# A PSUM column for an exclusive-or on VectorE, and ScalarE's one-hots in the plain parts of a graph layer

## The chip, the core and the metric

The kernel runs on one core of a Trainium2 chip. A core has five engines with queues of their own: TensorE (PE; its weight loads are listed as PEld), VectorE (DVE), ScalarE (ACT), GpSimd (POOL) and SyncE (SP, which issues most DMAs). Each works through its own instructions in order; semaphores tie them together. SBUF is the large on-chip memory of 128 partitions, PSUM the smaller one into which TensorE writes. The metric is the device time of one execution in microseconds.

## What is computed

A graph of 12500 nodes with 128 features each and 412500 directed edges, sorted by target node `dst` (200000 random pairs in both directions, and a loop at each node). For each edge the difference of its two nodes' rows is taken, a small network makes a gate of it, and gated differences are summed at the target:

```python
theta = x[dst] - x[src]
w = sigmoid(relu(theta @ W1 + b1) @ W2 + b2)
agg = segment_sum(w * theta, dst)
indeg = segment_sum(ones, dst)
y = agg + indeg * (x @ W4 + b4)
out = layernorm(x + y)
```

Since `theta @ W1` is `x[dst] @ W1 - x[src] @ W1`, a table of both products and rows can be made once, and an edge then needs one row of it, fetched by `src`.

## The kernel before

**Table.** The first stage (`chunk`, `table_chunk`) multiplies all rows by W1 and writes a table `z` to DRAM, a row being `x @ W1` and `x` side by side (1 KB).

**Sets.** Edges are worked in sets, one to a *part* of the program. Sets 0 to 17 are the *plain* sets of 1024 consecutive edges (`PLAIN = 18`, `K = 8` groups of 128 edges on the partitions); sets 0 to 3 (`NH = 4`) run on rows of `x` while the table is still being made. Sets 18 to 275 hold 1532 edges each; of those, up to 512 go by way of *hot* regions, and 1024 slots by gathers. For each set GpSimd issues eight gathers (`gather`, an indirect DMA of 128 rows, L401) into one of five buffers `zbuf`, four parts ahead in the plain parts and three in the later ones.

**A part.** VectorE takes the difference of the gathered half and the target's half (L948 in plain parts, L951 in later ones), clamps and multiplies by W2 (L956) and sums to logits `lg` (L962). ScalarE takes the sigmoid (L975) and weighs the rows (`weigh`, L986; `weigh_rest`, L993), which also frees the gather buffer. TensorE sums the weighed rows into windows of 104 target nodes (`add_up`, L1158), multiplying by one-hot matrices `ow` of the target's place in its window. `one_hot_w` (L926) makes these on VectorE, as `iota == rel`, two tiles of 4 x 104 columns for a plain set and one for a later set; four tiles `ow` exist. `iota` was copied to the PSUM tile `fix` at the start, as was W2 for L956. The places `rel` of the plain sets lie in the tile `rel0`, of BF16.

**Placement.** Which edges of a later set go to which hot region or gather slot is found on the chip by `place(i, ...)`, once for each of five groups of up to 64 sets (the last has two sets), with one list to a partition and 767 edges to a list. It goes through 32 regions (`HR`). For each it changes the bits of its keys by an exclusive-or with a constant (L583, 128x767, 31 times per group), takes the eight largest (`max`, L586), and marks them taken (L589). Further steps compact the lists (L640 to L682) and end in the indices `src_i` (L713, ScalarE), on which the gathers of these sets depend. `place` is a generator. `spend` and `advance` run some of its steps in each part, against a credit by part and a table of costs by kind of step, `"x": 0.5` for the exclusive-or. Group 0 (sets 18 to 81) is placed during the table stage and the plain parts and must be done before part 14 (`assert steps[0] is None`); groups 1 to 4 are placed one after the other in parts of the set group before.

**Hot tables.** In parts 4 to 9 `table_terms` (L1087, L1096) splits rows of `x` into three BF16 terms: once in parts 4 to 7, twice in parts 8 and 9. It goes through the PSUM banks `px` and `pd`. `place` uses the two `px` banks as scratch too (`where[0] = wide`), and both take them in turn. In later parts `hot_tiles` (L1039, VectorE) makes one-hots for the hot regions.

**Order.** From part 0 on, all of PE, DVE and ACT stand in the order in which `early_part` (plain parts) and `part` (later parts) write them. In `early_part` ScalarE gets, in this order: the copies of hot products (L1069), in odd parts the totals of a block (L1213, L820, L1232, L1234), whatever `logits` issues, the sigmoid, the weighting, in even parts the next block's plain one-hots (`plain_one_hots`, L860, L861), and the table terms.

Of the kernel before, what the change touches and what calls it, by code (L numbers as in the profile page):

```python
# [9 lines left out]
F32 = mybir.dt.float32  # L10
BF16 = mybir.dt.bfloat16
F16 = mybir.dt.float16
I32 = mybir.dt.int32
U16 = mybir.dt.uint16
AF = mybir.ActivationFunctionType
OP = mybir.AluOpType
# [4 lines left out]
P = 128  # L21
D = 128
K = 8
J = K // 2
BE = K * P
SUB = 2
WB = 104
# [12 lines left out]
NH = 4  # L40
# [3 lines left out]
PLAIN = FIRST + MORE  # L44
HS = 16
HR = 32
# [19 lines left out]
WL = HL + 1  # L66
# [7 lines left out]
FIELD = 19  # L74
# [10 lines left out]
def gnn_resnorm(  # L85
# [37 lines left out]
    nc = tc.nc  # L123
# [16 lines left out]
    while n0 < N:  # L140
# [5 lines left out]
    const = ctx.enter_context(tc.tile_pool(name="const", bufs=1))  # L146
# [8 lines left out]


    placed = {0: (const.tile([P, K, PLAIN], I32, name="src0"),
                  const.tile([P, K, PLAIN], BF16, name="rel0"), None)}

    def set_of(s):  # L160

        s0 = 0 if s < PLAIN else PLAIN + (s - PLAIN) // S2 * S2
        return placed[s0], s - s0
# [106 lines left out]
    iota_row = const.tile([P, P], F32, name="iota_row")  # L270
# [28 lines left out]
    fix = cps.tile([P, 512], F32, name="fix")  # L299
    iota_f = fix[:, :WB].rearrange("p (o m) -> p o m", o=1)  # L300
    w2_b = fix[:, WB:WB + D]
    w2_f = w2_r.rearrange("p (o m) -> p o m", o=1)

    oh_all = const.tile([P, NO * RW], F32, name="oh")
# [18 lines left out]
    def constants():  # L323

        nc.vector.tensor_copy(ident_b, ident)
        nc.vector.tensor_scalar_mul(nident_b, ident, -1.0)
        nc.vector.tensor_scalar_mul(wneg, wts[:, 0, :], -1.0)
        nc.scalar.activation(fix[:, :WB], iota_row[:, :WB], AF.Copy)

        nc.scalar.activation(w2_b, w2_r, AF.Copy)  # L330
        half = const.tile([P, 1], F32, name="half")
        nc.vector.tensor_scalar(half, iota_p, float(HALF), -float(HALF), op0=OP.is_ge, op1=OP.mult)
        nc.vector.tensor_add(half, half, iota_p)
        nc.vector.tensor_scalar(mine, half, float(SW), None, op0=OP.is_lt)
        nc.vector.tensor_scalar(away, half, float(SW), -2.0, op0=OP.is_gt, op1=OP.mult)
        nc.vector.tensor_mul(half, half, mine)
        nc.vector.tensor_sub(away, away, half)
        nc.vector.tensor_scalar_mul(less, mine, -1.0)

        nodes = const.tile([P, HT], F32, name="nodes")  # L340
        node_c = const.tile([P, 1], F32, name="node_c")
        nc.vector.tensor_scalar(node_c, iota_p, float(HT), None, op0=OP.mult)
        nc.vector.tensor_scalar(nodes, iota_row[:, :HT], node_c, None, op0=OP.add)

        most = const.tile([P, 1], F32, name="most")
        nc.vector.memset(most, float(SW + HKL))
        apart = const.tile([P, PM], F32, name="apart")
        nc.vector.tensor_scalar(apart, iota_row[:, :PM], float(HOT), None, op0=OP.mult)
        return nodes, (apart, most)
# [18 lines left out]
    def pairs(s):  # L368
        return J if s < NF else JT
# [130 lines left out]
    def place(i, scratch, es, ed, bb, dp):  # L500
# [4 lines left out]
        s0, n, full = sets[i]  # L505
# [3 lines left out]
        v = nc.vector  # L509
# [17 lines left out]
        for r in rows:  # L527
            v.scalar_tensor_tensor(b[r, 3:4], c[r, 2:3], float(NOT - WB + 1), c[r, 18:19],
                                   op0=OP.add, op1=OP.add)
# [39 lines left out]
        bits = left.bitcast(I32)  # L569
# [10 lines left out]
        tops = ep.tile([P, WL], F32, name="ed")[:, :HKL].rearrange("p (r e) -> p r e", e=HE)  # L580
        for r in range(HR):
            if r:
                v.tensor_scalar(bits, bits, ((r - 1) ^ r) << FIELD, None, op0=OP.bitwise_xor)  # L583
                yield "x"
            eight = tops[:, r, :]
            v.max(eight, left)  # L586
            v.tensor_scalar(eight, eight, FLOOR, None, op0=OP.max)
            yield "k"
            v.match_replace(left, eight, left, TAKEN)  # L589
            yield "k"  # L590
# [5 lines left out]
                        op0=OP.bitwise_xor, op1=OP.bitwise_and)  # L596
# [38 lines left out]
        for j in range(NC):  # L635
# [10 lines left out]
            else:  # L646
                v.memset(odd[:, :1], 0.0)
            v.tensor_tensor_scan(odd[:, 1:], mark, keep, c[:, 5:6] if j else 0.0,
                                 op0=OP.mult, op1=OP.add)
# [5 lines left out]
                                   op0=OP.min, op1=OP.mult)  # L655
# [18 lines left out]
        for r, m in enumerate([1 << r for r in range(MOVES)]):  # L674
            u = ep.tile([P, WL], I32, name="ew" if r % 2 else "et")
            for a in range(0, WL, P * G):
# [10 lines left out]
                        op0=OP.logical_shift_right, op1=OP.bitwise_and)  # L687
# [10 lines left out]
        rel = pp.tile([P, K, S2], BF16, name="rel")  # L698
# [20 lines left out]
    with tc.manual_schedule(engines={SP}), tc.tile_pool(name="work", bufs=2) as wp, tc.tile_pool(  # L719
        name="ps_y", bufs=2, space=bass.MemoryType.PSUM  # L720
    ) as ps_y, tc.tile_pool(
        name="ps_l", bufs=1, space=bass.MemoryType.PSUM
# [196 lines left out]
        def one_hot_w(s):  # L919

            (_, rel, _), i = set_of(s)
            n = pairs(s)
            parts[s]["ow"] = []
            for k0 in range(0, K if s < PLAIN else J, J):
                ow = wp.tile([P, J, WB], F32, name="ow", bufs=4)
                nc.vector.tensor_tensor(  # L926
                    ow[:, :n], iota_f.to_broadcast([P, n, WB]),
                    rel[:, k0:k0 + n, i:i + 1].to_broadcast([P, n, WB]), op=OP.is_equal)
                parts[s]["ow"].append(ow)

        def logits(s):
# [4 lines left out]
            if s < NH:  # L936
                one_hot_w(s)
                for i, h in enumerate(y):
                    w2 = w2_r.rearrange("p (o d) -> p o d", o=1).to_broadcast([P, J, D])
                    nc.vector.scalar_tensor_tensor(h, h, 0.0, w2, op0=OP.max, op1=OP.mult)  # L940
                    nc.vector.tensor_reduce(lg[:, i * J:(i + 1) * J, 0], h, AX.X, OP.add)
                return
# [16 lines left out]
            if s % SUB == 0:  # L959
                one_hot_w(s)  # L960
            for at in tiles:
                nc.vector.tensor_reduce(lg[:, at, 0], h[:, at, :], AX.X, OP.add)  # L962
            if s % SUB:
                one_hot_w(s)
# [343 lines left out]
        with after(done[1]):  # L1308
            place_first_dst(0, FIRST, ps_l, dst_f)
            nodes, hot_c = constants()  # L1310
            start_of(0, FIRST)

        where = [lambda: ps_l.tile([P, P * G], F32, name="pa")]
        steps = [place(0, lambda: where[0](), *loaded), "k"]

        def advance(kinds, n=1):
# [130 lines left out]
        groups, firsts, i = [], {}, 0  # L1447
# [47 lines left out]
        def part(s):  # L1495
# [6 lines left out]
            if s in edges:  # L1502
                i, loaded = edges.pop(s)
                assert steps[0] is None
                steps[:] = place(i, lambda: where[0](), *loaded), "k"
# [253 lines left out]
```

## Time and profile before

| | |
|---|---|
| Median of 3 runs (lowest to highest) | 2941.33 us (2940.52 to 2944.18) |
| Profiled execution | 2943.8 us |
| Its span, first to last instruction | 2942.0 us |
| VectorE busy | 2380.3 us (81%) |
| ScalarE busy | 2123.8 us (72%) |
| GpSimd busy | 2164.5 us (74%) |
| TensorE busy | 2548.2 us (87%) |
| First gather by placed indices | at 269.25 us |
| End of the last gather | 2915.45 us |

How to read the rows: a group's row has line, engine, operation, output<-inputs by tile names, shapes, `x` its count, then busy us, mean ns of one, and the idle time just before with what ended it. A row of the timeline has start, duration, engine, line, operation, and in brackets the idle time before it and its releaser. A row of waits has who waited for whom, total us, times, and the longest. A row of stretches has its length, then the busy time and count of PE, PEld, DVE, ACT and POOL, the granted TensorE clock, the DMA share and GB/s. A row of one line has the least, median and greatest duration in ns. "issue" is time for which the profile shows no releaser. A busy share says nothing on whether the gaps of an engine can be used.

### The profile page before, as it was taken

How to read it: one execution, taken by the hardware profiler on the slowest of the kernel's cores; microseconds unless marked ns; L12 is line 12 of the kernel's file. 1: busy time of each engine (PE TensorE's matmuls, PEld its weight loads, DVE VectorE, ACT ScalarE, POOL GpSimd, SP SyncE). 2: the span in 40 equal slices, each digit the busy share in tenths (PEclk: the TensorE clock that was granted, in tenths of full speed). 3: DMA queues.
4: the chain of work that ended last, by engine and by line, in shares of the span. 5: the costliest groups of instructions: out<-in, count | busy, mean ns of one | idle time of the engine just before them, and what ended most of it. 6: DMA issues, size and time to landing. Idle time of an engine off the chain costs nothing.

```text
span 2942.0 us, 59129 instructions
## 1 busy us (share of the span) xinstructions
PE 2548.2 (87%) x18606; PEld 2012.3 (68%) x18606; DVE 2380.3 (81%) x4436; ACT 2123.8 (72%) x6416; POOL 2164.5 (74%) x2213
## 2 busy tenths in 40 slices
PE   6877899988888998998898888898998888888886
PEld 5656677777676777776776666676776666677764
DVE  7899699888957988888558888888568888888654
ACT  6365778767777777677777777776777777677776
POOL 4566777777777777777777777777777777777774
PEclk8688999989999999999999999999999999999998
DMA  8455555555554555554554545454554555555542
GB/s 285 151 153 123 142 139 138 140 135 137 140 146 134 137 140 140 133 141 135 143 150 133 135 133 141 132 141 134 143 142 128 140 132 141 133 138 141 141 134 77
DMA packets 239329, 413.58 MB, mean 141 GB/s; under 512 B 63423, under 2 KB 147226, under 8 KB 237470
## 3 DMA queue, kind: packets, MB, share of 16 engines
q0 software_dynamic: 105280, 286.93, 35.3%
q1 hardware_dynamic: 131756, 116.40, 15.3%
q10 hardware_dynamic: 1970, 6.40, 0.7%
q8 instruction: 148, 2.42, 0.3%
q14 instruction: 175, 1.43, 0.2%
HBM read 388.57 MB, written 20.94 MB: 139 GB/s over the span
## 4 chain that ended last, share of the span: by engine, by line
PE 38%; ACT 19%; DVE 15%; DMA 11%; issue 7%; POOL 1%; DVEq 0%; SPq 0%; ACTq 0%; POOLq 0%
PE pa L1158 14%; DMA zbuf<-z,src_i 10%; DVE zbuf L951 5%; PE y L893 5%; PE pd L1055 5%; ACT wx L993 5%; PE px L1119 4%; ACT wxh L1131 4%; PE pz L1105 3%; PE pz L1106 3%; PE pz L1122 3%; ACT oh L872 2%; ACT oh L873 2%; ACT xT L1069 1%; ACT a L1213 1%
## 5 line engine op out<-in xcount | busy, mean ns | idle before, releaser
L401 POOL DMA_INDIRECT zbuf<-z,src_i x2060 | 2018.5, 980 | 637.0 <-issue 236.6
L993 ACT ACTIVATE wx<-zbuf,wx 128x128 f32<-128x128 f32 x2060 | 630.2, 388 | 0.0
L1158 PE MATMUL pa<-wx,ow 128*104 128x260 f32 (+1 forms) x2284 | 628.4, 393 | 0.0
L893 PEld LDWEIGHTS y<-y,oh 128*128 128x128 f32 (+1 forms) x2156 | 276.1, 197 | 420.5 <-DVE zbuf L951 378.2
L1055 PEld LDWEIGHTS <-tabs 128*128 128x128 bf16 x6360 | 452.8, 101 | 124.2 <-issue 8.2
L951 DVE TENSOR_TENSOR zbuf<-y,zbuf 128x1024 f32<-128x1024 f32 x258 | 315.1, 1221 | 272.2 <-DMA zbuf<-z,src_i 270.9
L1055 PE MATMUL pd<-of,tabs 128*128 128x128 bf16 (+3 forms) x6360 | 535.2, 223 | 0.0
L1111 ACT ACTIVATE hr<-pz 128x512 f32<-128x512 f32 x258 | 152.9, 593 | 522.9 <-PE pz L1106 522.8
L893 PE MATMUL y<-y,oh 128*128 128x128 f32 (+1 forms) x2156 | 314.7, 291 | 228.7 <-DVE zbuf L951 220.6
L1158 PEld LDWEIGHTS pa<-wx,ow 128*104 128x104 f32 x2284 | 342.8, 179 | 40.6 <-issue 0.4
L962 DVE TENSOR_REDUCE lg<-zbuf 128x8 f32<-128x1024 f32 x273 | 329.8, 1208 | 13.2
L956 DVE SCALAR_TENSOR_TENSOR zbuf<-zbuf,fix 128x1024 f32<-128x1024 f32 x273 | 331.6, 1215 | 9.3
L1158 PE MATMUL pa<-wxh,owh 128*104 128x130 f32 x2064 | 329.0, 296 | 0.0
L1131 ACT ACTIVATE wxh<-pz,wxh 128x128 f32<-128x128 f32 x1032 | 295.2, 369 | 42.1 <-PE pz L1122 35.9
L1105 PE MATMUL pz<-xT,wni 128*128 128x512 f32 x516 | 278.5, 621 | 1.6 <-ACT wxh L1131 1.6
L1158 PEld LDWEIGHTS pa<-wxh,owh 128*104 128x104 f32 x2064 | 274.3, 186 | 0.0
L1119 PEld LDWEIGHTS px<-w_c,hr 128*128 128x128 f32 x2064 | 263.5, 200 | 7.8 <-ACT hr L1111 7.8
L1119 PE MATMUL px<-w_c,hr 128*128 128x1 f32 x2064 | 262.1, 248 | 5.6 <-ACT hr L1111 5.6
L1106 PE MATMUL pz<-oh,y 128*128 128x512 f32 x516 | 264.5, 594 | 0.1
L872 ACT ACTIVATE oh<-to_all,away,mine 128x512 f32<-128x512 bf16 (+1 forms) x257 | 213.6, 831 | 3.1 <-DMA to_all<-off_d 3.1
L1106 PEld LDWEIGHTS pz<-oh,y 128*128 128x128 f32 x516 | 98.2, 191 | 124.3 <-issue 123.4
L1122 PE MATMUL pz<-wni,xT 128*128 128x128 f32 x1032 | 176.3, 297 | 0.0
(304 smaller groups left out, 3595.8 us busy)
## 6 DMA issues: line engine op xcount, KB each, us to landing
to_all<-off_d SPq DMA_DIRECT2D x258, 128.0 KB
zbuf<-z,src_i POOLq DMA_INDIRECT x2060
hot_src<-hot_s SPq DMA_DIRECT2D x228, 128.0 KB
y<-z SPq DMA_DIRECT2D x270, 28.0 KB
xw<-in_x_dram SPq DMA_DIRECT2D x138, 52.0 KB
out_dram<-o SPq DMA_DIRECT2D x138, 52.0 KB
wx<-in_x_dram ACTq DMA_DIRECT2D x12, 512.0 KB
z<-zbuf SPq DMA_DIRECT2D x6, 1024.0 KB
```

What stands on the lines that cost most here:

```text
L401: ins = nc.gpsimd.indirect_dma_start(out=rows_of(s)[:, k, :], out_offset=None, in_=z if s >= NH else x, in_offset=IndirectOffsetOnAxis(ap= ...
L893: nc.tensor.matmul(y[:, j, :], d["oh"][:, (k0 + j) * P:(k0 + j + 1) * P], y_of(s), start=True, stop=True)
L951: nc.vector.tensor_sub(half, yy.to_broadcast([P, 2, n, D]), half)
L956: nc.vector.scalar_tensor_tensor(h[:, at, :], h[:, at, :], 0.0, w2.to_broadcast([P, n, D]), op0=OP.max, op1=OP.mult)
L962: nc.vector.tensor_reduce(lg[:, at, 0], h[:, at, :], AX.X, OP.add)
L993: weighed[0] = nc.scalar.activation(wx[:, k, :D], rows_of(s)[:, k, D:], AF.Copy, scale=wx[:, k, D:D + 1])
L1055: steps_of.append(lambda q=q, i=i, t=t, j=j: nc.tensor.matmul(to[:, q], tabs[:, g, i, q, t, :], of[:, t, q], start=j == 0, stop=j == HT * ...
L1105: nc.tensor.matmul(pz, wneg, xT, start=True, stop=False)
L1106: nc.tensor.matmul(pz, y_of(t), blocks[t // SUB]["oh"][:, BP:], start=False, stop=True)
L1119: nc.tensor.matmul(lgh()[:, t % SUB, q:q + 1], hr[:, at], w2_c, start=True, stop=True)
L1131: nc.scalar.activation(wx[:, q, :D], pz[:, q * P:(q + 1) * P], AF.Copy, scale=wx[:, q, D:D + 1])
L1158: return [lambda i=i, one=one, w=w: nc.tensor.matmul(to if len(w.shape) == 3 else to[:, 0, :], one, w, start=first and i == 0, stop=last a ...
```

## The change

Two things are changed together.

*The exclusive-or.* In groups 1 to 4 of the placement (`if i:`) the instruction with a constant becomes one with two tensor operands, the second being one column of PSUM repeated along the row. Five such columns, with the five constants that occur (1, 3, 7, 15 and 31 shifted left by 19), are set once in the tile `fix`. Group 0 keeps the instruction with a constant. The table of costs is as before.

*One-hots of plain parts.* In sets 4 to 17 ScalarE makes them, as 1 - |rel - iota| clamped at zero: for each of the two tiles four instructions Abs, one to each group of 104 columns (the place `rel` is the bias by partition), and one Relu over the tile in place. `rel0` becomes F32. Sets 0 to 3 and all later sets keep VectorE's comparison.

```diff
     placed = {0: (const.tile([P, K, PLAIN], I32, name="src0"),
-                  const.tile([P, K, PLAIN], BF16, name="rel0"), None)}
+                  const.tile([P, K, PLAIN], F32, name="rel0"), None)}
...
+    steps_c = fix.bitcast(I32)[:, WB + D:WB + D + HR.bit_length() - 1]
...
+        for k in range(HR.bit_length() - 1):
+            nc.vector.memset(steps_c[:, k:k + 1], ((2 << k) - 1) << FIELD)
...
             if r:
-                v.tensor_scalar(bits, bits, ((r - 1) ^ r) << FIELD, None, op0=OP.bitwise_xor)
+                if i:
+                    k = ((r - 1) ^ r).bit_length() - 1
+                    v.tensor_tensor(bits, bits, steps_c[:, k:k + 1].to_broadcast([P, WL]), op=OP.bitwise_xor)
+                else:
+                    v.tensor_scalar(bits, bits, ((r - 1) ^ r) << FIELD, None, op0=OP.bitwise_xor)
                 yield "x"
...
-                nc.vector.tensor_tensor(
-                    ow[:, :n], iota_f.to_broadcast([P, n, WB]),
-                    rel[:, k0:k0 + n, i:i + 1].to_broadcast([P, n, WB]), op=OP.is_equal)
+                if NH <= s < PLAIN:
+                    for k in range(J):
+                        nc.scalar.activation(ow[:, k, :], iota_row[:, :WB], AF.Abs, scale=-1.0,
+                                             bias=rel[:, k0 + k, i:i + 1])
+                    nc.scalar.activation(ow, ow, AF.Relu, scale=-1.0, bias=1.0)
+                else:
+                    nc.vector.tensor_tensor(
+                        ow[:, :n], iota_f.to_broadcast([P, n, WB]),
+                        rel[:, k0:k0 + n, i:i + 1].to_broadcast([P, n, WB]), op=OP.is_equal)
```

## The prediction

> **What bounds the kernel now.** I read the page first (shares and the costliest groups), then GpSimd's own timeline, its waits, the stretches with and without exclusive-ors, and last the plain parts, engine by engine.
>
> ```profile
> span 2942.0 us, 59129 instructions
> PE 2548.2 (87%) x18606; PEld 2012.3 (68%) x18606; DVE 2380.3 (81%) x4436; ACT 2123.8 (72%) x6416; POOL 2164.5 (74%) x2213
> L401 POOL DMA_INDIRECT zbuf<-z,src_i x2060 | 2018.5, 980 | 637.0 <-issue 236.6 <-ACT wx L993 143.3 <-DMA zbuf<-z,src_i 61.3
> ```
>
> By shares TensorE would be the bound and POOL would have a quarter of its time free. The timeline of POOL says otherwise:
>
> ```profile
> 269.25 0.95 POOL L401 DMA_INDIRECT zbuf<-z,src_i  x1 [9.26 <-ACT src_i L713]
> ...
> 979.66 0.94 POOL L401 DMA_INDIRECT zbuf<-z,src_i  x1 [0.30 <-issue]
> ...
> 982.16 0.94 POOL L401 DMA_INDIRECT zbuf<-z,src_i  x1 [0.30 <-ACT hr L1111]
> 983.41 1.55 POOL L401 DMA_INDIRECT zbuf<-z,src_i  x1 [0.30 <-issue]
> ...
> 986.52 1.29 POOL L401 DMA_INDIRECT zbuf<-z,src_i  x1 [0.30 <-ACT sw L1232]
> ...
> 2914.50 0.95 POOL L401 DMA_INDIRECT zbuf<-z,src_i  x1 [0.30 <-issue]
> ```
>
> A gather takes 0.95 us and the next follows after 0.30, whoever is named as releaser. The same 0.30 stands in the waits as the longest wait on the engine that frees gather buffers:
>
> ```profile
> POOL zbuf L401 <- ACT wx L993: 143.3, 470, 0.3
> POOL zbuf L401 <- ACT src_i L713: 9.9, 3, 9.3
> DVE zbuf L951 <- DMA zbuf<-z,src_i: 270.9, 138, 6.5
> ```
>
> So from 269.25 us on POOL never waits for a buffer; VectorE waits for gathers, 138 times. 2060 gathers run from 269.25 to 2915.45 without a break: 2646.2 us, of which 2060 x 1.253 = 2581 is the undisturbed pace and 65 us is gathers that took longer than 0.95. A tail of 26.5 us follows. The time is thus: POOL's start at 269.25, plus 2581, plus 65, plus the tail. Only the first and the third can be moved by this change.
>
> **Who makes gathers longer.** VectorE beside those same gathers:
>
> ```profile
> 978.66 1.22 DVE L951 TENSOR_TENSOR zbuf<-y,zbuf 128x1024 f32<-128x1024 f32 x1
> 979.91 1.22 DVE L956 SCALAR_TENSOR_TENSOR zbuf<-zbuf,fix 128x1024 f32<-128x1024 f32 x1
> 983.07 0.61 DVE L1039 TENSOR_SCALAR of<-hot_src,nodes 128x512 bf16<-128x512 f16 x2
> 983.59 0.55 DVE L583 TENSOR_SCALAR ew<-ew 128x767 int32<-128x767 int32 x1
> 986.43 0.56 DVE L583 TENSOR_SCALAR ew<-ew 128x767 int32<-128x767 int32 x1
> ```
>
> The gather of 983.41 (1.55 us) meets L1039 and the exclusive-or L583; the gather of 986.52 (1.29) meets an L583 alone. Those beside L951 and L956, one operand of which lies in PSUM (y, fix), keep 0.94 to 0.95. The sum of it comes from the gathers' mean (ns, behind the busy time) in the four stretches that hold the later sets' exclusive-ors, 379 to 635, 946 to 1212, 1604 to 1868 and 2257 to 2530 us, and in two that hold none, 1270 to 1540 and 2590 to 2900:
>
> ```profile
> L401 POOL DMA_INDIRECT zbuf<-z,src_i x198 | 196.4, 992 | 60.3 <-issue 19.8 <-ACT wx L993 15.2 <-DMA zbuf<-z,src_i 5.8
> L401 POOL DMA_INDIRECT zbuf<-z,src_i x207 | 204.0, 985 | 63.1 <-issue 21.0 <-ACT wx L993 15.9 <-DMA zbuf<-z,src_i 6.1
> L401 POOL DMA_INDIRECT zbuf<-z,src_i x204 | 202.8, 994 | 62.2 <-issue 26.5 <-ACT wx L993 14.0 <-DMA zbuf<-z,src_i 5.2
> L401 POOL DMA_INDIRECT zbuf<-z,src_i x211 | 208.8, 990 | 64.3 <-issue 24.1 <-ACT wx L993 14.3 <-DMA zbuf<-z,src_i 6.7
> ...
> L401 POOL DMA_INDIRECT zbuf<-z,src_i x214 | 205.9, 962 | 65.3 <-issue 23.2 <-ACT wx L993 15.3 <-DMA zbuf<-z,src_i 7.3
> L401 POOL DMA_INDIRECT zbuf<-z,src_i x246 | 236.0, 959 | 75.0 <-issue 30.2 <-ACT wx L993 17.7 <-DMA zbuf<-z,src_i 4.3
> ```
>
> Against 960.5 the four are long by 31.5 x 198 + 24.5 x 207 + 33.5 x 204 + 29.5 x 211 ns = 24.4 us: what the later sets' 124 exclusive-ors cost POOL, 0.20 us each.
>
> **Part 1, the exclusive-or.** In sets 1 to 4 (4 x 31 = 124 instructions) a tensor-scalar on SBUF becomes a tensor-tensor whose second operand is one PSUM column. Its price on VectorE:
>
> ```profile
> L583 DVE TENSOR_SCALAR ew<-ew x155: 528/559/796, 37.4 to 2523.6; 128x767 int32<-128x767 int32 x155
> L577 DVE TENSOR_TENSOR ew<-ew,ed x5: 958/958/958, 33.2 to 2250.1; 128x767 int32<-128x767 int32 x5
> L926 DVE TENSOR_TENSOR ow<-fix,rel x294: 365/581/592, 22.0 to 2921.6; 128x416 f32<-128x416 f32 x147
> 379.00:635.00 256.00, 236.34 (x1778) 185.81 (x1776) 236.67 (x407) 198.26 (x620) 195.95 (x198) 0.97 0.51 138
> ```
>
> I take L577's 0.96 us, same shape and type; L926, with a PSUM and a repeated operand, lies on the same line (416 to 767 elements: 377 ns, 1.07 an element). So +0.40 each, 49 us of VectorE in all. It is hidden by VectorE's lead: in the first stretch it is busy 236.7 of 256 us (third number after the length) and gets 31 x 0.40 = 12.4 more, 249.1, while POOL's 198 gathers there need 256 - 6.2 = 249.8. That is as good as full, but the stretch contains VectorE's catching up; and POOL has buffers to run on: ScalarE frees one at 364.1 us that the gather of 373.48 is the first to need,
>
> ```profile
> 361.68 2.45 ACT L993 ACTIVATE wx<-zbuf,wx 128x128 f32<-128x128 f32 x8
> 373.48 0.95 POOL L401 DMA_INDIRECT zbuf<-z,src_i  x1 [0.30 <-DMA zbuf<-z,src_i]
> ```
>
> a slack of 9 us at the tightest place I found. If that cover were gone, each microsecond of VectorE over POOL's pace would be one of time. The other three stretches begin with more slack.
>
> POOL's gain has two ends. If the new form disturbs nothing, as L951 and L956 do not, it is 24.4, and up to 29 since the two stretches of reference hold later steps of placement and are themselves 14 ns over an undisturbed gather (12 us over the 820 gathers, of which I allow 5). If L1039, which stays, keeps the collisions that the two share, as in one of the two gathers shown, half is left, 12. If the second operand's place did not matter and the longer instruction blocked for longer, 0.96/0.56 of 24.4, it is a loss of 17. The new instruction resembles L956 most (one operand SBUF, one PSUM), so: **-24.4**.
>
> [...]
>
> Five one-column PSUM memsets in the constants cost some 0.1 us each on VectorE, and the F32 tile instead of BF16 nothing that a row would show; together I count them at nothing against the next term's width.
>
> **Part 2, one-hots of plain sets 4 to 17 on ScalarE.** Each part loses two tensor-tensors on VectorE (1.08 us, the next starts 1.0 later) and gains, twice, four Abs 128x104 and one Relu 128x416 on ScalarE.
>
> ```profile
> 235.64 1.08 DVE L926 TENSOR_TENSOR ow<-fix,rel 128x416 f32<-128x416 f32 x2
> L1153 ACT ACTIVATE sh<-lag,step_c x129: 362/366/402, 312.2 to 2921.8; 104x104 f32<-104x104 f32 x129
> L1154 ACT ACTIVATE sh<-sh x129: 289/289/292, 312.6 to 2922.2; 104x104 f32<-104x104 f32 x129
> L873 ACT ACTIVATE oh<-oh x257: 629/630/1057, 290.3 to 2893.4; 128x512 f32<-128x512 f32 x128, 128x1024 f32<-128x1024 f32 x1
> 130.00:270.00 140.00, 103.73 (x649) 80.42 (x648) 132.28 (x284) 82.17 (x197) 79.80 (x81) 0.80 0.50 135
> ACT wx L975 <- DVE lg L962: 47.9, 9, 9.8
> ```
>
> Abs is L1153's form; in a run such instructions start 0.28 apart (L993's eight in 2.45), so four take 3 x 0.28 + 0.37 = 1.2. Relu at 416, between 289 at 104 and 630 at 512, is 0.55. Per part 3.4 us, 14 parts 48 us. On VectorE, busy 132.3 of 140 us between 130 and 270, a part is shorter by 0.8 to 1.0.
>
> The wait for a free one-hot tile (four, freed by TensorE's sums of the part two before) moves from VectorE's queue to ScalarE's; behind it stand that part's sigmoid and weighting, for which TensorE's sums and the gather buffers wait. In ScalarE's order the sums it needs were issued a part earlier, so I count nothing for it up to part 15.
>
> Only one moment here counts: when set 0's indices (L713) let POOL start, 269.25. Up to there VectorE loses ten parts' one-hots (s = 4 to 13), 9 us, if nothing else holds it. ScalarE's cover is its waiting for the logits, 47.9 us in nine waits (row above) against 34 us up to part 13; but it isn't spread evenly. Around 211 to 222, where a part casts two groups of table terms (L1087, L1096), there is no such wait:
>
> ```profile
> 210.95 0.29 ACT L975 ACTIVATE wx<-lg,b_c 128x8 f32<-128x8 f32 x1
> ...
> 220.84 0.59 ACT L1096 ACTIVATE tabs<-px 128x512 bf16<-128x512 f32 x1
> ...
> 221.90 0.30 ACT L975 ACTIVATE wx<-lg,b_c 128x8 f32<-128x8 f32 x1
> ```
>
> These are the sigmoids (L975) of parts 9 and 10. I walked ScalarE's queue from part 4 on with 3.4 more before each sigmoid and every other duration as it is: the waits of parts 4 and 6 swallow what is added up to there, then parts 7, 8 and 9 add up, the sigmoid of part 9 comes 2.3 late, and the copy of 220.84 ends near 223.7 instead of 221.4. VectorE's next step of placement writes the same PSUM banks (px), so though it would by then be 4.5 us early, it is held to about 1 us later than now. After that it is free again, loses three more one-hots (2.8 us), and set 0's indices come **2 us** earlier. Ends: -9 (ScalarE holds nothing) and +6 (it also delays the last steps). Behind 269 the parts 14 to 17 keep ScalarE 3.4 us longer each; POOL has buffers, as shown.
>
> **Sum.** Span 2942.0 - 24.4 - 2 = 2915.6; the profiled execution took 2943.8, 1.8 around its span and 2.5 above the median of 2941.33. Taken off the median: 2941.3 - 26.4 = **2915 us**.
>
> **Rivals.**
> 1. *All of the relief counts* (ScalarE's one-hots always fit before the logits): -24.4 - 9, 2908 us. For it: nine waits of up to 9.8 us. Against it: the gapless run at 211 to 222. Chance 0.13.
> 2. *Slower: ScalarE sets the pace in the plain parts.* If its 3.4 us found no cover in parts 4 to 13, POOL would start 34 us later, and the result is 2941.3 - 24.4 + 34 = 2951. It decides against the change once 24.4 us are uncovered, seven of those parts, or at 5.8 us a part with four of them covered. Against it: ScalarE is busy 82.2 of the 140 us, so 57.8 are free for 34. Chance 0.06. The Trainium skill's page "ScalarE: Activation LUTs" (section "Rules for kernel authors") would leave relu, max and add to VectorE; by that rule this half of the change loses. Only its order of prices is borne out here: 3.4 us a part against 1.0.
> 3. *VectorE becomes the bound in the stretches of exclusive-ors*: 249.1 against 249.8 is near. The stretches then keep their length: near 2937. For it: the small distance in the first stretch. Against it: 240.0 of 267 and 234.8 of 268 in the next two, and the buffers. Chance 0.07.
> 4. *The change does not do what it says*: a two-operand instruction disturbs the gathers as much. Then only the 2 us remain, 2939. For it: L577 and its like, with both operands in SBUF, also stand beside long gathers. Against it: L951 and L956. Chance 0.07.
>
> ```profile
> 945.00:1212.00 267.00, 242.29 (x1790) 190.25 (x1789) 239.99 (x414) 203.53 (x627) 203.89 (x208) 0.95 0.51 137
> 1600.00:1868.00 268.00, 232.34 (x1770) 180.20 (x1769) 234.84 (x403) 197.53 (x612) 205.21 (x207) 0.98 0.50 136
> ```
>
> **How the numbers follow.** The forecast has 0.67, with a range of 2909 (29 us) to 2927 (12 us). The range that should hold 8 in 10 adds rival 1 and the plain term's upper end: 2904 to 2930. A measurement of this kernel tells about 0.2% (6 us) from no change: faster 0.86 (forecast, rival 1, part of 3), same 0.08 (rival 4 and part of 3), slower 0.06.
>
> **What would show it.** Right: the gathers' mean in the four stretches falls from 985-994 to about 960, L583's new form takes 0.96, POOL's longest wait after its start stays 0.3. POOL's first gather of set-0 indices starts near 267, and the sigmoids of parts 9 and 10 come later than now. Wrong: POOL waits on L993 for more than 0.3 (VectorE has run out of lead), gathers beside the new exclusive-or above 1.0 us, or a first gather behind 272.

## The result and the profile after

| | before | after |
|---|---|---|
| Median (lowest to highest), 4 runs each | 2940.93 us (2934.96 to 2944.18) | 2913.61 us (2912.77 to 2916.98) |
| Span of the profiled execution | 2942.0 us | 2915.2 us |
| First gather by placed indices | 269.25 us | 269.35 us |
| Busy time of the 2060 gathers | 2018.5 us | 1991.3 us |
| End of the last gather | 2915.45 us | 2887.88 us |

After to before is 0.9912 (0.9894 to 0.9929): 0.9% less, 27 us of medians. In the changed kernel the gather is L404, the exclusive-or L588 (groups 1 to 4) and L590 (group 0), the new one-hots L935 (Abs) and L937 (Relu), VectorE's difference L964, ScalarE's sigmoid L988, the weighting L1006, the copies of table terms L1109, `hot_tiles` L1052, the steps of placement L686, and the indices `src_i` L720.

From the page of the changed kernel, the busy times and the groups (busy us, mean ns | idle time before and what ended it):

```profile
span 2915.2 us, 59242 instructions
PE 2539.6 (87%) x18606; PEld 2005.0 (69%) x18606; DVE 2409.2 (83%) x4413; ACT 2167.7 (74%) x6556; POOL 2134.1 (73%) x2213
L404 POOL DMA_INDIRECT zbuf<-z,src_i x2060 | 1991.3, 967 | 634.1 <-issue 247.1
L964 DVE TENSOR_TENSOR zbuf<-y,zbuf 128x1024 f32<-128x1024 f32 x258 | 314.9, 1220 | 166.2 <-DMA zbuf<-z,src_i 164.6
```

The gathers' busy time fell from 2018.5 to 1991.3, by 27.2 us; the span fell by 26.8. VectorE got 29 us busier and waits 164.6 us for gathers where it waited 270.9: of these 106 us, 29 are now work, 27 are time saved, and the rest went into other waits. The timeline of POOL:

```profile
261.60 0.95 POOL L404 DMA_INDIRECT zbuf<-z,src  x1 [0.30 <-ACT ow L935]
269.35 0.94 POOL L404 DMA_INDIRECT zbuf<-z,src_i  x1 [6.80 <-ACT src_i L720]
...
2886.93 0.95 POOL L404 DMA_INDIRECT zbuf<-z,src_i  x1 [0.30 <-issue]
```

and its waits (total us, times, longest):

```profile
POOL zbuf L404 <- ACT wx L1006: 141.4, 464, 0.3
```

POOL starts at the same moment as before, and from there on never waits longer than 0.3 us: it still sets the pace. The gathers' group in the four stretches that hold the exclusive-ors of the later sets, 379 to 635, 946 to 1212, 1604 to 1868 and 2257 to 2530 us:

```profile
L404 POOL DMA_INDIRECT zbuf<-z,src_i x203 | 195.6, 963 | 61.9 <-issue 24.7 <-ACT wx L1006 13.4 <-DMA zbuf<-z,src_i 5.8
L404 POOL DMA_INDIRECT zbuf<-z,src_i x211 | 203.3, 964 | 64.3 <-issue 23.5 <-ACT wx L1006 14.6 <-DMA zbuf<-z,src_i 4.6
L404 POOL DMA_INDIRECT zbuf<-z,src_i x209 | 201.2, 962 | 63.7 <-issue 26.2 <-ACT wx L1006 15.5 <-DMA zbuf<-z,src_i 3.7
L404 POOL DMA_INDIRECT zbuf<-z,src_i x215 | 207.8, 966 | 65.5 <-issue 26.8 <-ACT wx L1006 14.9 <-DMA zbuf<-z,src_i 5.5
```

The means were 992, 985, 994 and 990 ns. They are now 962 to 966, close to what the stretches without exclusive-ors had. The lines of the new instructions (least, median, greatest ns):

```profile
L588 DVE TENSOR_TENSOR ew<-ew,fix x124: 934/953/954, 384.2 to 2497.7; 128x767 int32<-128x767 int32 x124
L935 ACT ACTIVATE ow<-iota_row,rel x112: 349/366/422, 137.7 to 299.3; 128x104 f32<-128x104 f32 x112
L937 ACT ACTIVATE ow<-ow x28: 549/550/552, 138.9 to 299.7; 128x416 f32<-128x416 f32 x28
```

So the gain lies in the gathers, and the plain parts' lighter VectorE (busy 132.3 us before and 124.3 after, between 130 and 270 us) did not bring POOL's start forward.

### The profile page after: what moved, and what is told of

It is laid out like the page before. It is cut to its first block, busy times and chain, and to the rows that moved or that the text cites. A ratio compares the mean times of both kernels' runs of the same rounds, so it can differ in the third digit from the quotient of the medians.

```text
span 2915.2 us, 59242 instructions
## 1 busy us (share of the span) xinstructions
PE 2539.6 (87%) x18606; PEld 2005.0 (69%) x18606; DVE 2409.2 (83%) x4413; ACT 2167.7 (74%) x6556; POOL 2134.1 (73%) x2213
## 4 chain that ended last, share of the span: by engine, by line
PE 39%; ACT 22%; DVE 20%; DMA 10%; issue 8%; POOL 1%; DVEq 0%; ACTq 0%; SPq 0%; POOLq 0%
PE pa L1171 13%; DMA zbuf<-z,src_i 9%; DVE zbuf L964 6%; PE y L900 5%; PE pd L1068 5%; ACT wx L1006 4%; PE px L1132 4%; ACT wxh L1144 3%; PE pz L1118 3%; PE pz L1119 3%; PE pz L1135 3%; ACT oh L879 2%; ACT oh L880 2%; ACT xT L1082 2%; DVE ed L593 1%
## 5 line engine op out<-in xcount | busy, mean ns | idle before, releaser
L404 POOL DMA_INDIRECT zbuf<-z,src_i x2060 | 1991.3, 967 | 634.1 <-issue 247.1
L1006 ACT ACTIVATE wx<-zbuf,wx 128x128 f32<-128x128 f32 x2060 | 630.3, 388 | 0.0
L1171 PE MATMUL pa<-wx,ow 128*104 128x260 f32 (+1 forms) x2284 | 622.5, 390 | 0.0
L964 DVE TENSOR_TENSOR zbuf<-y,zbuf 128x1024 f32<-128x1024 f32 x258 | 314.9, 1220 | 166.2 <-DMA zbuf<-z,src_i 164.6
L1171 PEld LDWEIGHTS pa<-wx,ow 128*104 128x104 f32 x2284 | 338.2, 177 | 40.8
L1171 PE MATMUL pa<-wxh,owh 128*104 128x130 f32 x2064 | 326.9, 295 | 0.0
L1171 PEld LDWEIGHTS pa<-wxh,owh 128*104 128x104 f32 x2064 | 272.1, 185 | 0.0
```

The costliest lines, as they stand in the source:

```text
L404: ins = nc.gpsimd.indirect_dma_start(out=rows_of(s)[:, k, :], out_offset=None, in_=z if s >= NH else x, in_offset=IndirectOffsetOnAxis(ap= ...
L964: nc.vector.tensor_sub(half, yy.to_broadcast([P, 2, n, D]), half)
L1006: weighed[0] = nc.scalar.activation(wx[:, k, :D], rows_of(s)[:, k, D:], AF.Copy, scale=wx[:, k, D:D + 1])
L1171: return [lambda i=i, one=one, w=w: nc.tensor.matmul(to if len(w.shape) == 3 else to[:, 0, :], one, w, start=first and i == 0, stop=last a ...
```

## The experiments

The chips differ. On some of them the kernel before took 2941 to 2943 us. On the chips of eight of the runs below it took 4049 to 4120, and there the gathers do not set the pace; those runs stand by themselves at the end.

### Each half alone

The exclusive-or alone, with VectorE's one-hots and the BF16 `rel0`:

```diff
-                if NH <= s < PLAIN:
+                if False:
```

> The exclusive-or alone, again, since on the chip of the first run the kernel before took 4057 us and GpSimd was not its pace. Where the kernel before takes about 2941 us. My theory (the gathers set the pace, and what the old exclusive-or added to them is all of the gain): gathers' mean in the four stretches near 962 ns, first gather by placed indices between 268 and 272 us, 2912 to 2918 us, ratio 0.990 to 0.993. Rival (the plain parts bring half or more of the gain): ratio 0.995 or more.

Measured: 2921.07 us, ratio 0.9929 (0.9915 to 0.9943), span 2916.4; by the ratio 21 us less (17 to 25). Its gathers, from its page:

```profile
L404 POOL DMA_INDIRECT zbuf<-z,src_i x2060 | 1992.8, 967 | 636.5 <-issue 247.1
```

They take 25.7 us less than before, and the first stands at 270.19 us. The ratio, the means in the four stretches (960 to 969 ns) and the first gather came as expected; the time lies 3 us above the expected range. This half carries most of the gain.

The one-hots alone, without columns and memsets:

```diff
-                if i:
+                if False:
                     k = ((r - 1) ^ r).bit_length() - 1
```

> The plain sets' one-hots on ScalarE alone, again where GpSimd is the pace. My theory: VectorE's relief is held up by ScalarE's copies out of the px banks, POOL's first gather by placed indices comes at 266 to 271 us, gathers in the four stretches stay at 985 to 994 ns, 2936 to 2943 us, ratio 0.998 to 1.001. Rival (the plain parts bring a quarter of the gain, 7 us): first gather at 262, ratio 0.9975 or less.

Measured: 2937.95 us, ratio 0.9994 (0.9984 to 1.0004), so between 5 us less and 1 us more. From its page:

```profile
L401 POOL DMA_INDIRECT zbuf<-z,src_i x2060 | 2014.5, 978 | 634.2 <-issue 250.7
```

The gathers keep their length but for 4 us (986 to 993 ns in the four stretches), and the first stands at 268.83, all as expected. The ratios of the halves multiply to 0.9923, inside the interval of the whole change: nothing shows that they help or hinder each other.

### The same instruction with its column in SBUF

Two theories fit the gain so far: that the second operand's place in PSUM leaves GpSimd undisturbed, or that any form with two tensor operands does, wherever they lie. Only the columns' place is changed:

```diff
-    steps_c = fix.bitcast(I32)[:, WB + D:WB + D + HR.bit_length() - 1]
+    steps_c = const.tile([P, HR.bit_length() - 1], I32, name="steps")
```

> The whole change with its five columns in SBUF, again, for the same reason. My theory (the operand in PSUM is what frees the gathers; with two SBUF operands the longer instruction delays them as the old one did or more): gathers' mean in the four stretches 985 to 1010 ns, 2937 to 2962 us. Rival (any two-operand instruction is harmless, only the short form blocks): near 962 ns, 2912 to 2917 us.

Measured: 2963.57 us, ratio 1.0057 (1.0037 to 1.0077): slower than before, on the same chip and beside the same runs of before as the exclusive-or alone. The time is 1.6 us above the expected range, and the means in the four stretches (1001, 1010, 1008 and 1018 ns) reach above theirs. The line of the instruction and, from the page, the gathers:

```profile
L588 DVE TENSOR_TENSOR ew<-ew,steps x124: 936/957/960, 386.0 to 2543.9; 128x767 int32<-128x767 int32 x124
```

```profile
L404 POOL DMA_INDIRECT zbuf<-z,src_i x2060 | 2036.5, 989 | 634.0 <-issue 239.6
```

The instruction is as long as with PSUM (957 against 953 ns), but the gathers take 45.2 us more than in the changed kernel, 0.36 us for each of 124. The form before, of 0.56 us, cost 27.2, which is 0.22 each. The timeline shows single cases, in this kernel

```profile
990.78 0.96 DVE L588 TENSOR_TENSOR ew<-ew,steps 128x767 int32<-128x767 int32 x1
1008.86 0.96 DVE L588 TENSOR_TENSOR ew<-ew,steps 128x767 int32<-128x767 int32 x1
```

```profile
990.87 1.70 POOL L404 DMA_INDIRECT zbuf<-z,src_i  x1 [0.30 <-ACT wx L1006]
1009.14 1.50 POOL L404 DMA_INDIRECT zbuf<-z,src_i  x1 [0.30 <-issue]
```

and in the changed kernel, where a long gather goes with L1052 and none with a lone L588:

```profile
979.51 0.95 DVE L588 TENSOR_TENSOR ew<-ew,fix 128x767 int32<-128x767 int32 x1
...
989.69 0.95 DVE L588 TENSOR_TENSOR ew<-ew,fix 128x767 int32<-128x767 int32 x1
994.97 0.61 DVE L1052 TENSOR_SCALAR of<-hot_src,nodes 128x512 bf16<-128x512 f16 x2
```

```profile
994.95 1.44 POOL L404 DMA_INDIRECT zbuf<-z,src_i  x1 [0.30 <-ACT oh L879]
```

With the column in SBUF both gathers end 0.83 and 0.82 us after the L588 that they met (992.57 and 991.74, 1010.64 and 1009.82 us).

The timelines of VectorE and POOL from 370 to 2600 us show that these cases are the rule. Take the gathers whose first 0.95 us run beside one of the 124 exclusive-ors and beside no `hot_tiles` (L1039, L1052). Held, that is longer than 1.0 us, are 60 of 108 in the kernel before, none of 130 in the changed kernel, none of 117 in the exclusive-or alone, and 91 of 152 with the column in SBUF. Which of them are held depends on when the instruction runs:

| the exclusive-or | before | PSUM column | SBUF column |
|---|---|---|---|
| began before the gather, still runs 0.19 us into it | 42 of 42 held | 0 of 82 | 91 of 91 held |
| began 0.34 to 0.51 us into the gather | 18 of 18 held | 0 of 7 | 0 of 21 |

In the first row a held gather ends 0.82 us after the exclusive-or, in the second 0.12 us after it. So the old form holds a gather at two of its moments, the form with both operands in SBUF at one, and the form with the PSUM column at none. The PSUM operand is the cause, and the rival "any two-operand form" has fallen.

### The one-hots of parts 7 to 10 left to VectorE

```diff
-                if NH <= s < PLAIN:
+                if NH <= s < PLAIN and s not in (7, 8, 9, 10):
```

> The whole change, but the one-hots of parts 7 to 10, where ScalarE has no wait for logits, are left to VectorE. My theory (the relief is lost where ScalarE is full: its copies of the table terms hold the px banks that VectorE's placement needs): VectorE's waits on those copies, 3.9 and 2.9 us in the profile of the change, get shorter by 3 us or more together, first gather by placed indices 3 to 5 us earlier, 264 to 267 us, 2908 to 2912 us. Rival (something else sets that moment, such as the loads of the hot indices, or VectorE's whole length): first gather no earlier than 268, and 2913 to 2918 us.

Measured: 2913.23 us, ratio 0.9909 (0.9895 to 0.9924), span 2910.3. POOL's start in its timeline:

```profile
264.88 0.95 POOL L404 DMA_INDIRECT zbuf<-z,src_i  x1 [8.28 <-ACT src_i L720]
```

The first gather came in the expected range, the time did not: it lies 1 us above, in the range of the rival. In the profiled execution six parts' relief of VectorE before that moment (4 to 6 and 11 to 13) bring 4.4 us against the kernel before, where ten parts' brought none. Why, is seen in the changed kernel's waits of VectorE between 130 and 270 us,

```profile
DVE px L654 <- ACT tabs L1109: 3.9, 1, 3.9
DVE px L686 <- ACT tabs L1109: 2.9, 1, 2.9
DVE of L1052 <- DMA hot_src<-hot_s: 2.9, 1, 2.9
```

against a single one in this variant, as in the kernel before (where it was 2.2):

```profile
DVE px L654 <- ACT tabs L1109: 2.7, 1, 2.7
```

VectorE's waits on the copies fall from 6.8 us to 2.7, by more than the 3 expected. The 8.0 us by which VectorE is less busy in these 140 us of the changed kernel are nearly all there as additional waiting for the copies and for `hot_src`, 7.5 us (9.7 against 2.2). In time the variant can't be told from the changed kernel: the intervals of the two ratios lie on each other, and the profiled execution of the changed kernel was the longest of its four. That the 4.4 us last in the time is not shown.

### On the chips of 4050 us

There the kernel before took 4057.30, 4049.38 and 4119.70 us in three groups of runs. Beside the kernels above four more edits ran, and one of them (`e6`) twice. The column in group 0 too (`e4`):

```diff
-                if i:
+                if True:
```

the exclusive-or three times in a row, which undoes itself and applies once (`e6`):

```diff
+                    for _ in range(3):
-                    v.tensor_tensor(bits, bits, steps_c[:, k:k + 1].to_broadcast([P, WL]), op=OP.bitwise_xor)
+                        v.tensor_tensor(bits, bits, steps_c[:, k:k + 1].to_broadcast([P, WL]), op=OP.bitwise_xor)
```

and one table term more in part 4 and one less in part 8 (`e7`), with the one-hots of parts 8 to 10 left to VectorE besides (`e8`):

```diff
-        made = {4: (0,), 5: (1,), 6: (2,), 7: (3,), 8: (4, 5), 9: (6, 7)}
+        made = {4: (0, 1), 5: (2,), 6: (3,), 7: (4,), 8: (5,), 9: (6, 7)}
```

> Only the exclusive-or by a PSUM column; the plain sets' one-hots stay on VectorE and rel0 in BF16. My theory (the gathers set the pace, and what the old exclusive-or added to them is all of the gain): the gathers' mean in the four stretches near 962 ns as with the whole change, POOL's first gather by placed indices between 268 and 272 us, time 2913 to 2918 us. Rival (the plain parts bring half or more of the gain): 2927 us or more, with a first gather no earlier than now and gathers as long as before in some stretches.

> Only the plain sets' one-hots on ScalarE; the exclusive-or as before. My theory: POOL's first gather by placed indices stays between 266 and 271 us, since VectorE's relief is held up by ScalarE's copies out of the px banks; gathers in the four stretches stay at 985 to 994 ns; time 2936 to 2943 us. Rival (the plain parts bring half of the gain): first gather near 256 us, 2927 us.

> The whole change, but the five columns lie in SBUF instead of PSUM; the instruction is as long. My theory (it is the second operand from SBUF, or the two-element mode, that keeps gathers waiting, and PSUM is what frees them): gathers' mean in the four stretches 985 to 1010 ns again, 24 to 48 us slower than with the change, 2937 to 2962 us. Rival (a two-operand instruction is harmless whatever its operands, only the short form of the old one blocks): gathers near 962 ns, 2913 to 2917 us.

> The whole change, and the exclusive-or by a PSUM column in set group 0 too, 31 instructions of 0.40 us more while VectorE is full and POOL isn't the pace: 12.4 us, of which VectorE's waits behind the table terms (3.9 and 2.9 us in the profile of the change) can swallow half. My theory: first gather by placed indices at 274 to 281 us, time 2919 to 2926 us. Rival (VectorE's length before that gather does not matter either, since ScalarE or the table stage sets its time): first gather at 269 to 271, 2913 to 2916 us.

> In the sets after the first the exclusive-or with the PSUM column is issued three times in a row instead of once (the column undoes itself, so the result is the same): 248 more instructions of 0.95 us on VectorE, about 62 us more in each of the four stretches. Theory (the instruction with one operand in PSUM disturbs no gather; POOL sets the pace only as long as VectorE keeps its lead): the gathers' mean in the four stretches stays at 960 to 970 ns where POOL does not wait, but VectorE, busy 246 to 260 of 256 to 273 us there, has no room for 62 more; POOL now waits for weighted buffers by more than 0.3 us, and the time is 2950 to 3060 us. Rival (VectorE's time is free in these stretches, POOL sets the pace whatever VectorE does): 2911 to 2918 us, longest wait 0.3. Second rival (what is left of the lengthened gathers comes from this instruction too): the gathers' mean rises above 980 ns.

> The changed kernel with one table term more in part 4, where ScalarE waits 5.65 us for logits, and one less in part 8; the one-hots stay as changed. Theory (the plain parts' relief is lost because ScalarE has no idle time before the sigmoids of parts 7 to 11 and VectorE waits for its copies of table terms): first gather at 262 to 267 us instead of 269.3, time 2906 to 2912 us. Rival (VectorE waits for something else, such as the hot_src transfer): first gather at 268 to 271 us, 2911 to 2916 us.

> The changed kernel with one table term more in part 4 and one less in part 8, and with the one-hots of parts 8, 9 and 10 left to VectorE. Theory (each microsecond by which ScalarE's copies come earlier lets VectorE go on, down to VectorE's own work): first gather at 259 to 264 us, 2903 to 2910 us, faster than with the one-hots of parts 7 to 10 left alone (first gather at 264.9, 2913.2 us). Rival (that variant is already bound by VectorE's own work): first gather at 264 to 266 us, 2910 to 2914 us.

> In the sets after the first the exclusive-or with the PSUM column is issued three times in a row instead of once (the column undoes itself): 248 more instructions of 0.95 us on VectorE, about 62 us more in each of the four stretches, of which VectorE has 10 to 20 us free (busy 246 to 260 of 256 to 273 us in the changed kernel). Theory (the instruction with one operand in PSUM disturbs no gather; POOL sets the pace only while VectorE keeps its lead): the gathers' mean stays at 960 to 970 ns, VectorE falls behind by 42 to 52 us in each stretch, buffers cover 10 to 40 us of that, and POOL now waits for weighted buffers by more than 0.3 us: 2945 to 3060 us. Rival (POOL sets the pace whatever VectorE does in these stretches, so the term of 49 us on VectorE was free in any amount): 2911 to 2918 us, longest wait of POOL 0.3. Second rival (what is left of the lengthened gathers comes from this instruction too): the mean rises above 980 ns.

| kernel | us | ratio to before | gathers' mean, ns | first gather, us |
|---|---|---|---|---|
| e1, exclusive-or alone | 4045.03 | 0.9947 (0.9913 to 0.9982) | 956 | 309.1 |
| e2, one-hots alone | 4066.28 | 1.0018 (0.9986 to 1.0051) | 966 | 323.1 |
| e3, columns in SBUF | 4053.08 | 1.0006 (0.9966 to 1.0047) | 977 | 320.0 |
| e4, column in group 0 too | 4056.21 | 0.9989 (0.9956 to 1.0022) | 956 | 318.3 |
| e6, exclusive-or thrice | 4048.73 | 0.9982 (0.9948 to 1.0016) | 955 | 315.5 |
| e7, table terms earlier | 4046.03 | 0.9988 (0.9957 to 1.0020) | 958 | 313.3 |
| e8, and parts 8 to 10 left | 4040.92 | 0.9979 (0.9943 to 1.0016) | 959 | 308.0 |

The second run of e6, on a third such chip, gave 4102.33 against 4119.70, with runs too far apart for a ratio. No expectation in microseconds held here: all were made for a chip on which gathers set the pace. That they do not set it here is seen in the exclusive-or alone, the same kernel that took 2921 above. From its page, the busy times, the chain that ended last and the gathers:

```profile
PE 3015.6 (74%) x18602; PEld 2298.0 (56%) x18606; DVE 2430.9 (60%) x4441; ACT 2134.9 (52%) x6416; POOL 2112.2 (52%) x2213
...
PE 47%; issue 20%; ACT 15%; another core or an unknown queue 11%; DVE 5%; DMA 1%; DVEq 0%; POOL 0%; ACTq 0%; POOLq 0%; SPq 0%
...
L404 POOL DMA_INDIRECT zbuf<-z,src_i x2060 | 1970.0, 956 | 1738.7 <-ACT wx L1006 1219.6
```

and from its waits:

```profile
PE pa L1171 <- issue: 314.6, 374, 2.1
```

TensorE runs at a granted clock of 0.83, against 0.94 above, and stands where the profile shows nothing that it waits for: before the sums of L1171 374 times, 0.84 us on average and 2.1 at most. On the chip of 2921 us no such row is among TensorE's nine longest waits. POOL waits 1220 us for ScalarE's weighting, which frees its buffers. The profiles of e2, e3 and e6 show the same (18 or 19% of issue on the chain, 1137 to 1187 us of that wait). What holds TensorE there stays open.

Two things can still be read. First, the gathers' lengths keep their order without the time: 966 with the form before, 977 with both operands in SBUF, 955 or 956 with the PSUM column. The exclusive-or thrice is the sharpest of these:

```profile
span 4050.2 us, 59486 instructions
PE 3011.7 (74%) x18602; PEld 2278.4 (56%) x18606; DVE 2650.9 (65%) x4661; ACT 2177.9 (54%) x6556; POOL 2110.1 (52%) x2213
...
L404 POOL DMA_INDIRECT zbuf<-z,src_i x2060 | 1968.1, 955 | 1717.0 <-ACT wx L1007 1186.7
```

248 more of the instructions, 220 us of VectorE more than in the exclusive-or alone (2430.9), and the gathers are as short as with 124: nothing shows that these instructions disturb a gather. Second, the kernels that have all of the new one-hots (e2, e3, e4, both runs of e6, and e7 with moved terms) start POOL at 312.1 to 323.1, the two with fewer or none (e8, e1) at 308.0 and 309.1. That is the order of the theory, but weak, with one execution of each: the sigmoid of part 2 alone stands anywhere from 145.3 us (e8) to 152.8 (e2), and counted from it e8 and the second run of e6 are alike (162.7 and 162.9 us).

Not settled: what the column in group 0 would cost, how much VectorE work beyond the 49 us would stay hidden, and whether moved table terms gain anything. These would need a chip on which POOL sets the pace.

## Why the prediction was right

**What bounds the kernel.** Right. POOL's start, the undisturbed pace, the lengthened gathers and the tail give the time of both kernels: the start moved by 0.1 us, the gathers' length by 27.2, the tail from 26.6 to 27.3, and the longest wait stayed 0.3.

**The exclusive-or, -24.4 us.** Right in mechanism and nearly in size. The four stretches' means fell by 29, 21, 32 and 24 ns, which over the 820 gathers of before is 21.7 us; the gathers' total fell by 27.2, and alone by 25.7. The one-hots alone have 4.0 of such a fall without any change to the exclusive-or, so 22 to 27 us belong to this term. The end of +17, for the case that the second operand's place did not matter, was worked out as 0.96/0.56 of the collisions. The kernel with the columns in SBUF is that case: its gathers took 18.0 us more than before. That the two agree so well is partly luck: the working made the same collisions longer, but the old form held 60 lone gathers at two moments, the new one 91 at one, each for longer.

The Trainium skill's page "SBUF — State Buffer" (section "SBUF: two separate sides") states that VectorE and GpSimd share a port pair under an exclusive lock, that a VectorE instruction in a two-port mode keeps GpSimd from writing a DMA's descriptors, that one with two SBUF inputs contends only with a GpSimd instruction that reads SBUF, and that one with at most one SBUF input, outside those modes, does not contend. It infers that a `tensor_tensor` leaves the writing of descriptors alone. The trace agrees as far as the PSUM column held none of 130 gathers, and two SBUF inputs held them at one moment where the tensor-scalar did at two. No run shows which moment is a read and which the writing of descriptors, or that L583 ran in a two-port mode. Two SBUF inputs are not harmless for gathers, though: they cost 45.2 us here.

**VectorE's price, 0.96 us each, hidden.** Right: 0.953 us. VectorE was busy 246.4 of 256 us in the first stretch (249.1 was worked out), and POOL's longest wait stayed 0.3. Rival 3 did not come.

**The one-hots' price.** Right: 0.366 and 0.550 us against 0.37 and 0.55, so 3.4 us a part. Rival 2 did not come, as the one-hots alone lose nothing that shows.

**The plain parts, -2 us.** The mechanism came as described, its steps were larger than worked out. From the timelines of the kernel before, ScalarE and VectorE:

```profile
127.27 0.30 ACT L975 ACTIVATE xT<-lg,b_c 128x8 f32<-128x8 f32 x1
...
216.70 0.59 ACT L1096 ACTIVATE tabs<-px 128x512 bf16<-128x512 f32 x1
```

```profile
220.65 0.67 DVE L679 TENSOR_SCALAR px<-et 128x512 int32<-128x512 int32 x1
```

and of the changed kernel:

```profile
128.56 0.30 ACT L988 ACTIVATE xT<-lg,b_c 128x8 f32<-128x8 f32 x1
...
217.00 0.29 ACT L988 ACTIVATE wx<-lg,b_c 128x8 f32<-128x8 f32 x1
...
223.12 0.59 ACT L1109 ACTIVATE tabs<-px 128x512 bf16<-128x512 f32 x1
...
231.88 0.29 ACT L988 ACTIVATE wx<-lg,b_c 128x8 f32<-128x8 f32 x1
```

```profile
215.36 0.61 DVE L1052 TENSOR_SCALAR of<-hot_src,nodes 128x512 bf16<-128x512 f16 x2 [2.92 <-DMA hot_src<-hot_s]
...
223.75 0.69 DVE L686 TENSOR_SCALAR px<-et 128x512 int32<-128x512 int32 x1 [2.93 <-ACT tabs L1109]
```

The step that failed is the walk along ScalarE's queue. It had the sigmoid of part 9 come 2.3 us late; it came 6.1 late (217.00 for 210.95), and that of part 10 came 10.0 late. 1.3 of this was there before any new one-hot (the sigmoid of part 2, 128.56 for 127.27). The copy that held VectorE was not the one of 220.84 but that of part 9's first group, at 216.70 before and 223.12 after, 6.4 late. So the step of placement behind it came 3.1 us late (223.75 for 220.65), not 1. From there the three one-hots of parts 11 to 13 gave back 3.0, as worked out (2.8), and POOL started 0.1 us later than before instead of 2 earlier. Without the 1.3 us the sigmoid of part 9 is 4.8 late, the step 1.8, and POOL starts 1.2 earlier: the walk was still short, by 2.5 us at part 9, and which wait it took too large stays open. The wait for `hot_src` at 215.36 was not foreseen; it cost nothing of its own, since the wait for the copy ends behind it.

How early a program reaches part 2 differs between executions, so the start is better counted from there. From the sigmoid of part 2 to the first gather the kernels with all of the new one-hots take 140.8, 140.5 and 141.3 us (the changed kernel, the one-hots alone, the column in SBUF), those with none 142.0 and 143.2 (before, the exclusive-or alone). By these single executions the one-hots bring POOL's start forward by 1 to 3 us, near the 2 that were predicted.

In time the one-hot half is worth between 5 us less and 1 more by the runs, which agrees with -2 and with nothing. In the profiled execution the start did not move, and the gathers brought 2.8 us more than the term that the prediction gave them. That the sum of -26.4 came out at -27.3 by medians is partly luck: two small errors of opposite sign. Two side sums of the prediction do not come out: the range's lower end is 2910 us (2941.3 - 29 - 2), not 2909, and with four of ten parts covered rival 2 turns the change into a loss at 4.1 us a part (24.4 over six parts), not 5.8. Neither bears on the outcome.

**Rival 1** (all of the relief counts, first gather at 260) did not come; leaving four parts to VectorE, where POOL started 4.4 us earlier in the profiled execution, agrees with the account that the relief is there and that ScalarE's lack of idle time in parts 7 to 10 takes it back. **Rival 4** (the operand's place does not matter) is refuted by the columns in SBUF. **The memsets** and the F32 tile, counted at nothing: the five memsets take 0.06 us each (L333), and no effect can be told apart, since the sigmoid of part 2 comes at 127.0 to 129.9 us in executions with memsets and at 127.3 and 128.4 in those without.

## What to carry to other kernels

Find the engine that goes without a break, and ask what makes its single instructions longer; here a slower VectorE instruction made the kernel faster, since VectorE had time and GpSimd's gathers had none. Moving one operand of this instruction into PSUM took it out of the gathers' way, for 0.39 us more of VectorE each time, and a kernel with the same instruction on SBUF alone is the test of that reason. Work given to an engine "with free time" must fit where that engine waits: follow its queue part by part, adding its start shift and all that piles up, for a share of busy time doesn't show where the gaps are.

## What was not expected of the hardware

- Two tensor operands in SBUF hold up the gathers too, by 0.36 us on average for 0.957 us of instruction, against 0.22 for the tensor-scalar of 0.559 us. A gather that begins under either ends 0.82 us after it; only the tensor-scalar also holds a gather that it meets halfway (18 of 18 against 0 of 21).
- The same kernel takes 2921 us on one chip and 4045 on another. The gathers do not set the pace there, as POOL waits 1220 us for its buffers; TensorE has a granted clock of 0.83 instead of 0.94 and stalls without a visible releaser, 315 us in 374 pieces before L1171 alone. What shorter gathers are worth there is not shown: the exclusive-or alone has 0.9947 (0.9913 to 0.9982), but e4, e6, e7 and e8, with gathers as short, have 0.9979 to 0.9989 with intervals that hold 1.
